# Order of the first loads in a two-layer attention and mixture-of-experts kernel

## Chip, core and metric

The kernel runs on one core of a Trainium2 chip. The metric is the device time of one execution in microseconds (us). The kernel before took 1843.43 us, the median of three runs (1840.93 to 1843.54).

## The reference, cut to what matters

Two layers run one after the other over 8 x 100 tokens of 512 features, all in float32. Each has cross attention to a context (722 rows for each of the 8 batches, 512 features) and a feed-forward part with 8 experts, of which every token takes 2. Only the first attention's beginning bears on the change:

```python
x = x + _L0_xattn_ref(_layernorm(x, axis=-1), ctx_1024, q_w, q_b, k_w, k_b, v_w, v_b, o_w, o_b)
# in _L0_xattn_ref(x, context, ...): 16 heads of 32
q = x @ q_w + q_b
k = context @ k_w + k_b
v = context @ v_w + v_b
att = einsum('bhtd,bhsd->bhts', q, k) / sqrt(32)
att = where(tril(ones((T, S))), att, -inf)      # causal: only the first 100 context rows count
y = einsum('bhts,bhsd->bhtd', softmax(att), v)
return y @ o_w + o_b
...
# then the experts of layer 0, attention of layer 1 (all 722 context rows), the experts of layer 1
```

Since a token sees at most the first 100 context rows in this first attention, the keys and values need only those rows.

## The kernel before, in words

The tokens lie in one tile `x`, in seven tiles of rows: the first holds 32, the other six 128 each. The context is handed over feature by feature, so that one piece of 128 features of the first 100 rows of all batches (`cT[:, dc]`, four pieces, 400 KB each) is 128 partitions with 8 runs of 100 numbers, 400 bytes each. The weights `k_w`, `q_w`, `v_w`, `o_w` are handed over so that each is one load of 128 partitions with 8 KB each (1 MB); they go through a ring of eight tiles (`Weights`, L43 to L63), whose loads all stand in SP's queue.

Instructions are issued by five engines, each in its own order; a planner (the tile framework's scheduler) lays out that order from the order of the program and the dependencies. A load is issued by the engine that the program names: SP and ACT have a hardware queue each, POOL (GpSimd) a software queue. In the order of the program:

- The tokens come first, in ACT's queue (L106 to L109): tile 0, tile 1, tiles 2 and 3, tiles 4 to 6.
- Constants follow: the identity, `eps`, `rank` and so on.
- In the first attention (from L515), the four pieces of `cT` go to SP, SP, POOL, POOL (L519, L520), then the four weights to SP (L522), then the small parameters through POOL (L523 to L529). Two of these are wide: `v_b` and `o_b`, spread over 128 partitions, 256 KB each (L524, helper L162).
- POOL then makes the mask and `nil`, a tile of zeros (L531 to L534). SP fills two tables in memory, `sent` and `answers`, with these zeros, 25 loads of 512 KB each (L535 to L543), with the loads of `Wm` and of the first context for later stages among them (L542, L544).
- TensorE begins with two parts of the key columns (`columns(0, 2)` and `columns(0, 3)`, L606 and L607; helper `columns_part`, L454): each sums four chunks `dc` of `cT` and `k_w`, and ScalarE evicts each with the bias `k_b` (L556).
- The seven token tiles are then normalised (L608 to L612): VectorE makes the moments (L133, L135), ScalarE the root (L153), VectorE the reciprocal, the shift and the scaled tile `xn` (L154, L156, L160), TensorE transposes it (L171), ScalarE copies it to `xT` (L173), and POOL adds `o_b` to `x` (L612).
- Two parts of the query columns follow (L613), and then the 32 units of the first attention (L627), with values, scores and softmax.

Of the kernel before, what the change touches and what calls it, by code (L numbers as in the profile page):

```python
# [8 lines left out]
F32 = mybir.dt.float32  # L9
# [4 lines left out]
P = 128  # L14
D = 512
# [4 lines left out]
NTILE = -(-NT // P)  # L20
# [19 lines left out]
SHORT = NT - NT // P * P  # L40
# [26 lines left out]
def two_layers(ctx: ExitStack, tc: tile.TileContext, a: dict, out: bass.AP):  # L67
    nc = tc.nc
    x_in = a["x"].rearrange("b t d -> (b t) d")
    y_out = out.rearrange("b t d -> (b t) d")  # L70
    rows = [SHORT] + [P] * (NTILE - 1)
    starts = [0] + list(range(SHORT, NT, P))
# [30 lines left out]

    x = const.tile([P, NTILE, D], F32, name="x")
    nc.vector.memset(x[:, 0, :], 0.0)
    nc.scalar.dma_start(out=x[:SHORT, 0, :], in_=x_in[:SHORT])  # L106
    for i0, i1 in ((1, 2), (2, 4), (4, NTILE)):
        of_tiles = x_in[starts[i0] : starts[i0] + (i1 - i0) * P]
        nc.scalar.dma_start(out=x[:, i0:i1, :], in_=of_tiles.rearrange("(i p) d -> p i d", p=P))  # L109

    ident = const.tile([P, P], F32, name="ident")
    make_identity(nc, ident)
# [12 lines left out]
    def param(name, shape, pool=const):  # L125
        t = pool.tile(shape, F32, name=f"p_{name}")
        nc.gpsimd.dma_start(out=t, in_=a[name])
        return t
# [9 lines left out]
    def factors(mv, tag, twice=False, by_power=False):  # L138


        r = small.tile([P, 1], F32, tag=f"r{tag}", name=f"r{tag}")
        if by_power:
            if twice:
                nc.gpsimd.tensor_scalar(r, mv[:, 1:], 1.0 + EPS, EPS * EPS, ALU.mult, ALU.add)
                nc.gpsimd.tensor_tensor(r, r, half, ALU.pow)
            else:
                nc.gpsimd.tensor_scalar(r, mv[:, 1:], EPS, None, ALU.add)
                nc.gpsimd.tensor_tensor(r, r, half, ALU.pow)
        else:
            if twice:  # L150
                nc.scalar.activation(r, mv[:, 1:], AF.Sqrt, bias=eps2, scale=1.0 + EPS)
            else:
                nc.scalar.activation(r, mv[:, 1:], AF.Sqrt, bias=eps)  # L153
            nc.vector.reciprocal(r, r)  # L154
        t = small.tile([P, 1], F32, tag=f"t{tag}", name=f"t{tag}")
        nc.vector.scalar_tensor_tensor(t, mv[:, :1], -1.0, r, ALU.mult, ALU.mult)  # L156
        return r, t
# [4 lines left out]
    def broadcast(name, shape, pool, tag):  # L162
        t = pool.tile(shape, F32, tag=tag, name=f"p_{name}")
        nc.gpsimd.dma_start(out=t, in_=a[name].partition_broadcast(P))
        return t
# [349 lines left out]
    with tc.tile_pool(name="a0", bufs=1) as ap, tc.tile_pool(name="a0w", bufs=3) as aw, tc.tile_pool(  # L515
        name="a0s", bufs=1, space=bass.MemoryType.PSUM
    ) as ps_s, tc.tile_pool(name="a0p", bufs=2, space=bass.MemoryType.PSUM) as ps:
        cT = ap.tile([P, DC, B, T], F32, tag="cT", name="cT")
        for dc, queue in enumerate((nc.sync, nc.sync, nc.gpsimd, nc.gpsimd)):  # L519
            queue.dma_start(out=cT[:, dc], in_=a["ctxT"][dc * P : (dc + 1) * P, :, :T])  # L520
        cTf = cT.rearrange("p c b t -> p c (b t)")
        w_k, w_q, w_v, w_o = (weights.get(k, 0) for k in range(4))  # L522
        q_b, k_b = param("q_b", [P, DC], ap), param("k_b", [P, DC], ap)  # L523
        v_b, o_b = broadcast("v_b", [P, D], ap, "v_b"), broadcast("o_b", [P, D], ap, "o_b")  # L524
        gamma0, beta0 = param("gamma", [P, DC]), param("beta", [P, DC])
        wg0, bg0 = param("Wg", [P, DC, NE]), param("bg", [1, NE])
        b1 = param("b1", [P, NE, F0 // P])
# [139 lines left out]
        for i in range(NTILE):  # L667
# [9 lines left out]
            r, t = factors(mv, "a")  # L677
# [35 lines left out]
    with f0, tc.tile_pool(name="f0w", bufs=2) as fw, tc.tile_pool(  # L713
        name="f0p", bufs=2, space=bass.MemoryType.PSUM
# [89 lines left out]
    with tc.tile_pool(name="a1", bufs=1) as ap, ExitStack() as later, tc.tile_pool(  # L804
        name="a1s", bufs=1, space=bass.MemoryType.PSUM
# [3 lines left out]
        w_q, w_k, w_v, w_m, w_o = (  # L809
            [weights.get(W_L1A + 2 * n + g, 0) for g in range(2)] for n in (0, 2, 3, 1, 4)  # L810
        )
# [158 lines left out]
        for i in range(NTILE):  # L970
            n = min(t0 + T for t0 in range(0, NT, T) if t0 + T >= starts[i] + rows[i]) // T * IC + 2
# [27 lines left out]
    with tc.tile_pool(name="f1", bufs=1) as fp, tc.tile_pool(name="f1w", bufs=2) as fw, tc.tile_pool(  # L999
        name="f1p", bufs=2, space=bass.MemoryType.PSUM  # L1000
# [150 lines left out]
```

## Time and profile before

| what | us |
|---|---|
| median of three runs | 1843.43 |
| the profiled execution's own time | 1848.14 |
| its span, from the first to the last instruction | 1846.2 |
| TensorE's matmuls busy (PE) | 1725.2, 93% of the span |
| VectorE (DVE), ScalarE (ACT), GpSimd (POOL) busy | 584.5, 458.1, 167.7 |
| last matmul of the first two key parts issued | 26.9 |
| first transposes of the tokens | 28.74 |

The profile is one execution taken by the hardware profiler; its times are from the start of the span. PE is TensorE's matmuls, PEld its loading of weights, SPq, ACTq and POOLq are the issuing of loads. A group such as `L459 PE MATMUL ps_col<-cT,w` names the line, engine, operation and tiles; each matmul of the program in float32 shows as two. The memory queues are named by number: q1 is SP's, q10 ACT's, q0 POOL's. In the share of 16 engines, 100% means that all sixteen memory engines of the core worked for the whole window.

### The profile page before, as it was taken

The numbers are of one execution on the slowest core, as the hardware profiler recorded it, in microseconds if no ns is written. First come the engines' busy times: TensorE is split into PE (matmuls) and PEld (weight loads), VectorE is DVE, ScalarE is ACT, GpSimd is POOL, SyncE is SP. The second block draws the span as 40 slices with busy tenths as digits, with TensorE's granted clock in tenths as the row PEclk, the third lists the DMA queues.
The fourth block names the chain that finished last, engine by engine and source line by source line (L and its number), as shares of the span: only waits on it lengthen the run. The fifth ranks groups of instructions, "written<-read, shape, count | busy, mean of one in ns | idle before, by whom it ended". The sixth has DMA issues, their size and how long they took to land.

```text
span 1846.2 us, 26502 instructions
## 1 busy us (share of the span) xinstructions
PE 1725.2 (93%) x10427; PEld 1306.3 (71%) x10427; DVE 584.5 (32%) x1489; ACT 458.1 (25%) x1370; POOL 167.7 (9%) x283
## 2 busy tenths in 40 slices
PE   4999899999999979999999999999999959999990
PEld 2455578999999845666666656666666649999990
DVE  3464520110111140355444414444444411111115
ACT  2365321111111131333333323323233310010110
POOL 4010210000000150000010000000000010030003
PEclk9999899999999989999999999999999979999995
DMA  9921284454555563032120110213010265465513
GB/s 368 413 76 58 81 336 168 168 191 173 201 199 223 186 212 135 25 98 65 33 71 5 7 33 7 38 16 49 5 6 4 28 227 196 163 222 200 197 59 116
DMA packets 74422, 233.32 MB, mean 126 GB/s; under 512 B 23178, under 2 KB 35582, under 8 KB 57894
## 3 DMA queue, kind: packets, MB, share of 16 engines
q1 hardware_dynamic: 52978, 183.42, 28.8%
q0 software_dynamic: 10128, 30.84, 5.2%
q10 hardware_dynamic: 11172, 17.17, 3.1%
q8 instruction: 86, 1.41, 0.3%
q14 instruction: 58, 0.48, 0.1%
HBM read 180.36 MB, written 51.04 MB: 125 GB/s over the span
## 4 chain that ended last, share of the span: by engine, by line
PE 62%; issue 15%; DMA 7%; POOL 1%; DVE 1%; ACT 1%; POOLq 0%; ACTq 0%; another core or an unknown queue 0%; SPq 0%; DVEq 0%
PE ps_m L470 14%; PE ps_h L734 10%; PE ps_y L399 9%; PE ps_sc L852 5%; PE ps_col L459 5%; PE ps_av L902 4%; PE ps_v L934 3%; PE ps_ptA L881 3%; DMA answers<-y 3%; PE ps_o L950 3%; PE ps_mv L482 2%; DMA firsts<-answers,where 1%; DMA back<-answers,where 1%; PE ps_tp L171 1%; ACT pr L858 1%
## 5 line engine op out<-in xcount | busy, mean ns | idle before, releaser
L470 PE MATMUL ps_m<-cb,w 128*128 128x361 f32 x896 | 297.5, 483 | 0.0
L399 PE MATMUL ps_y<-h,w 128*128 128x256 f32 (+7 forms) x1536 | 280.5, 344 | 0.0
L399 PEld LDWEIGHTS ps_y<-h,w 128*128 128x128 f32 x1536 | 268.6, 190 | 7.9
L470 PEld LDWEIGHTS ps_m<-cb,w 128*128 128x128 f32 x896 | 169.2, 194 | 102.5 <-issue 14.4
L734 PE MATMUL ps_h<-xgT,w 128*128 128x256 f32 (+7 forms) x1024 | 188.4, 345 | 0.0
L734 PEld LDWEIGHTS ps_h<-xgT,w 128*128 128x128 f32 x1024 | 179.9, 191 | 5.6 <-ACT h L738 0.2
L858 ACT ACTIVATE pr<-ps_sc,m 100x822 f32<-100x822 f32 x128 | 120.0, 943 | 187.8 <-DVE m L856 95.1
L856 DVE TENSOR_REDUCE m<-ps_sc 100x1 f32<-100x822 f32 x128 | 123.8, 1009 | 46.5 <-PE ps_sc L852 46.5
L474 ACT COPY mT<-ps_m 128x361 f32<-128x361 f32 x128 | 58.8, 462 | 311.1 <-PE ps_m L470 276.5
L882 DVE COPY prT<-ps_ptA 128x500 f32<-128x500 f32 x128 | 82.1, 678 | 168.4 <-PE ps_ptA L881 168.4
L738 ACT ACTIVATE h<-ps_h,s_b 128x256 f32<-128x256 f32 (+7 forms) x128 | 56.1, 439 | 303.5 <-PE ps_h L734 303.5
L459 PE MATMUL ps_col<-xT,w 128*128 128x400 f32 x320 | 113.2, 511 | 1.6 <-ACT xT L180 1.6
L1033 PE MATMUL ps_g<-xgT,w 128*128 128x256 f32 (+7 forms) x512 | 104.4, 347 | 0.0
L1033 PE MATMUL ps_u<-xgT,w 128*128 128x256 f32 (+7 forms) x512 | 102.8, 344 | 0.0
L459 PEld LDWEIGHTS ps_col<-xT,w 128*128 128x128 f32 x320 | 61.2, 195 | 46.9 <-issue 2.5
L1033 PEld LDWEIGHTS ps_g<-xgT,w 128*128 128x128 f32 x512 | 91.3, 192 | 3.0
L852 PE MATMUL ps_sc<-mT,qT 64*100 64x311 f32 (+1 forms) x512 | 93.1, 468 | 0.0
L1033 PEld LDWEIGHTS ps_u<-xgT,w 128*128 128x128 f32 x512 | 90.8, 190 | 2.7
L902 PEld LDWEIGHTS ps_av<-prT,mv 128*64 128x64 f32 (+1 forms) x1536 | 67.9, 137 | 27.1 <-issue 24.7
L1038 ACT ACTIVATE sg<-ps_g 128x256 f32<-128x256 f32 (+7 forms) x64 | 22.3, 349 | 238.8 <-PE ps_g L1033 238.8
L902 PE MATMUL ps_av<-prT,mv 128*64 128x100 f32 (+1 forms) x1536 | 80.6, 253 | 0.0
L881 PEld LDWEIGHTS ps_ptA<-ident,pr 100*128 100x128 f32 x640 | 65.2, 141 | 20.7 <-issue 10.5
(274 smaller groups left out, 1824.2 us busy)
## 6 DMA issues: line engine op xcount, KB each, us to landing
w<-in_W SPq DMA_DIRECT2D x64, 1024.0 KB
w<-in_w_gate SPq DMA_DIRECT2D x16, 1024.0 KB
w<-in_w_up SPq DMA_DIRECT2D x16, 1024.0 KB
w<-in_w_down SPq DMA_DIRECT2D x16, 1024.0 KB
sent<-nil SPq DMA_DIRECT2D x25, 512.0 KB
answers<-nil SPq DMA_DIRECT2D x25, 512.0 KB
cb<-in_ctxT ACTq DMA_DIRECT2D x16, 722.0 KB
mT<-kept_keys SPq DMA_DIRECT2D x13, 361.0 KB
```

The costliest lines, as they stand in the source:

```text
L399: nc.tensor.matmul(py[:, k, :n], ws[f // 4][:, f % 4, dc * P : (dc + 1) * P], h[:, f, :n], start=f == 0, stop=f == nf - 1,)
L459: nc.tensor.matmul(ps[:, :HALF], w[c // 4][:, dc, (c % 4) * P : (c % 4 + 1) * P], xT[:, dc, cols], start=dc == 0, stop=dc == DC - 1,)
L470: nc.tensor.matmul(pm[:, : S // 2], w_m[ic // 4][:, dc, (ic % 4) * P : (ic % 4 + 1) * P], cb[h][:, dc, : S // 2], start=dc == 0, stop=dc = ...
L474: nc.scalar.copy(mT[:, h * (S // 2) : (h + 1) * (S // 2)], pm[:, : S // 2])
L734: nc.tensor.matmul(ph[:, :n], w[:, dc, j * P : (j + 1) * P], xg[:, dc, :n], start=dc == 0, stop=dc == DC - 1,)
L852: nc.tensor.matmul(sc[:, bank, c0:c1], qT[r, ic, q0 : q0 + T], keys_, start=True, stop=True)
L856: nc.vector.tensor_reduce(m, sc[:, :, :NKH], AX.XY, ALU.max, negate=True)
L858: nc.scalar.activation(pr.rearrange("p (a n) -> p a n", a=2), sc[:, :, :NKH], AF.Exp, bias=m, accum_out=sums[:, j : j + 1],)
L881: nc.tensor.transpose(pt[:, c, :], pr[:, T + c * P : T + (c + 1) * P], ident[:T, :T])
L882: nc.vector.tensor_copy(prT[:, : NSC - 1, :], pt)
L902: nc.tensor.matmul(po[r, 0, :], vj, prT[j][:w, c, :], start=c == 0, stop=c == NSC)
L1033: nc.tensor.matmul(p_[:, :n], w_[:, dc, j * P : (j + 1) * P], xg[:, dc, :n], start=dc == 0, stop=dc == DC - 1,)
```

## The change

```diff
 x = const.tile([P, NTILE, D], F32, name="x")
 nc.vector.memset(x[:, 0, :], 0.0)
-nc.scalar.dma_start(out=x[:SHORT, 0, :], in_=x_in[:SHORT])
-for i0, i1 in ((1, 2), (2, 4), (4, NTILE)):
-    of_tiles = x_in[starts[i0] : starts[i0] + (i1 - i0) * P]
-    nc.scalar.dma_start(out=x[:, i0:i1, :], in_=of_tiles.rearrange("(i p) d -> p i d", p=P))
...
 cT = ap.tile([P, DC, B, T], F32, tag="cT", name="cT")
-for dc, queue in enumerate((nc.sync, nc.sync, nc.gpsimd, nc.gpsimd)):
+for dc, queue in enumerate((nc.sync, nc.scalar, nc.scalar, nc.scalar)):
     queue.dma_start(out=cT[:, dc], in_=a["ctxT"][dc * P : (dc + 1) * P, :, :T])
+nc.scalar.dma_start(out=x[:SHORT, 0, :], in_=x_in[:SHORT])
+for i0, i1 in ((1, 2), (2, 4), (4, NTILE)):
+    of_tiles = x_in[starts[i0] : starts[i0] + (i1 - i0) * P]
+    nc.scalar.dma_start(out=x[:, i0:i1, :], in_=of_tiles.rearrange("(i p) d -> p i d", p=P))
 cTf = cT.rearrange("p c b t -> p c (b t)")
 w_k, w_q, w_v, w_o = (weights.get(k, 0) for k in range(4))
 q_b, k_b = param("q_b", [P, DC], ap), param("k_b", [P, DC], ap)
-v_b, o_b = broadcast("v_b", [P, D], ap, "v_b"), broadcast("o_b", [P, D], ap, "o_b")
+v_b, o_b = (ap.tile([P, D], F32, tag=n, name=f"p_{n}") for n in ("v_b", "o_b"))
+for t, n in ((v_b, "v_b"), (o_b, "o_b")):
+    nc.gpsimd.tensor_copy(t[:1, :1], w_k[:1, 0, :1])
+    nc.gpsimd.dma_start(out=t, in_=a[n].partition_broadcast(P))
```

The first context piece stays in SP's queue, ahead of the weights; the other three go to ACT's queue, and the tokens behind them there. POOL's queue carries no context any more. The loads of `v_b` and `o_b` get a one-element copy from `k_w` ahead of them on POOL, which writes into the tile that the load fills: so each of the two loads waits until `k_w` has landed. What is computed stays the same.

The planner lays out the changed program with further differences: on ACT, the two evictions of the key columns stand ahead of all roots of the layer norm (before, five roots stood ahead of them), with one more table load between the evictions and the first root; on SP, the first piece of `Wm` stands behind the 25 fills of `sent` (before, ahead of them); the load of tokens 2 and 3 waits for `cT[:, 0]` and that of tokens 4 to 6 for `cT[:, 2]`, since they share semaphores with these.

## The prediction

> **What bounds the kernel now.** I read the page first, for the whole, and then only the first 46 us, since every edited line issues a first load. The row of slices, with the page's head:
>
> ```profile
> span 1846.2 us, 26502 instructions
> ...
> PE   4999899999999979999999999999999959999990
> ...
> PE 62%; issue 15%; DMA 7%; POOL 1%; DVE 1%; ACT 1%; POOLq 0%; ACTq 0%; another core or an unknown queue 0%; SPq 0%; DVEq 0%
> ```
>
> A slice is 46 us; in the first one TensorE is busy four tenths, and from then on nearly always. So the start is a stretch in which TensorE stands still, and from 36 us on (windows 36 to 46, 46 to 56 and 56 to 100 us show it 10.00, 9.94 and 43.93 us busy) it is the bound: a microsecond won or lost before 36.05 us is a microsecond of the end, unless a later wait eats it. The waits of the first 45 us, and then the order of time there:
>
> ```profile
> ACT ra L153 <- DVE mv_a L135: 20.3, 3, 10.5
> DVE st_a L133 <- DMA x<-in_x: 18.9, 3, 8.5
> PE ps_col L459 <- DMA w<-in_k_w: 18.8, 1, 18.8
> ```
>
> ```profile
> 3.28 1.28 ACT L153 ACT_TABLE_LOAD   x1 [3.28 <-DVE sel L235]
> ...
> 18.77 8.59 PE L459 MATMUL ps_col<-cT,w 128*128 128x400 f32 x16 [18.77 <-DMA w<-in_k_w]
> ...
> 25.81 0.69 DVE L133 BATCH_NORM_STATS2 st_a<-x 128x6 f32<-128x512 f32 x1 [7.71 <-DMA x<-in_x]
> ...
> 28.07 1.06 ACT L556 ACTIVATE kT<-ps_col,p_k_b 128x400 f32<-128x400 f32 x2
> ...
> 36.05 6.72 PE L459 MATMUL ps_col<-xT,w 128*128 128x400 f32 x16
> ```
>
> The columns are start, duration, engine, line, operation; in brackets the idle time and its end. The first view has total, times, longest: VectorE waits for tokens in three pieces, ScalarE for the moments that VectorE makes of them. TensorE waits 18.77 us for the keys' weights, makes the key columns until 27.36, then follows the layer norm of the seven token tiles (their last load landed at 25.8), and at 36.05 starts the query columns. **36.05 us is the number to move.** What shares the memory engines meanwhile:
>
> ```profile
> ## 3 DMA queue, kind: packets, MB, share of 16 engines
> q0 software_dynamic: 94, 0.34, 51.7%
> q10 hardware_dynamic: 102, 0.21, 32.9%
> q1 hardware_dynamic: 104, 0.10, 16.9%
> ```
>
> ```profile
> q1 hardware_dynamic: 201, 1.47, 90.9%
> ```
>
> ```profile
> q1 hardware_dynamic: 648, 0.25, 110.0%
> ```
>
> These are the queues between 7 and 9 us, SP's own queue (q1) between 20 and 24, and q1 between 4 and 5. In the first, three queues hold work, POOL's with records of some 4 KB, ACT's (q10) with 2 KB, SP's mostly with the 400-byte rows of cT, and each got the same number of records, about 100: **the turn goes by record, not by byte.** From the other two comes the price of a record on one of the 16 engines: 400 bytes 1.10 x 16 us / 648 = 27 ns; 8 KB 0.909 x 64 us / (1.47 MB / 8192) = 0.324 us.
>
> **The change, part by part.** A piece of cT is 128 x 8 rows of 400 bytes, so 64 records per engine; a weight matrix is 128 rows of 8 KB, so 8.
>
> *Context pieces.* Before, SP carried two and POOL two. Now SP carries cT0, then k_w, q_w, v_w, o_w; ACT carries cT1, cT2, cT3, then the tokens. In the changed program's order v_w waits for cT1's landing and o_w for k_w's, both early, so SP's queue does not run dry. Data start to flow at about 3 us (the rates by time show 46 GB/s up to 3 us, 280 after). cT0 and cT1 take turns: 128 x 27 ns = 3.5 us, to 6.5. Then k_w: 8 turns of 0.324 + 0.027 = 2.8 us, to 9.3, seen by TensorE at about 10. So far the plan holds, 8.7 us sooner than 18.77. But q_w, v_w and o_w follow with no wait, and for each of their 24 turns cT2 gets one 400-byte row. By the time SP's 32 big records are through, ACT's queue has moved 32 of its 128 rows. cT3 is in when everything ahead has gone: 256 x 27 ns = 6.9, 32 x 0.324 = 10.4, and v_b and o_b (0.52 MB, by the same price per byte) 1.3, in all 18.6; from 3 us that is 21.6, and with the way to the semaphore 22.5. cT2 comes 64 x 27 ns = 1.7 us earlier, at 20.8. Bounds: 12.5 us if nothing overtakes (3 + 6.9 + 8 x 0.324, all pieces and k_w alone), 25.8 if the slowest engine lags as it did for the last tokens.
>
> Here a rule is weighed. The Trainium skill (DMA: Bandwidth & Descriptors, Queues, rings and completion order) says an engine drains a whole packet, some 9 to 17 descriptors, from one row's ring before it turns to the next. With 13 rows for each 8 KB turn, cT2 and cT3 (128 rows) would need 10 turns, 10 x (0.324 + 13 x 0.027) = 6.8 us, and land at 13.3. POOL's 4 KB records in the trace look like such bundles; the hardware queues' 400-byte records do not, 104 against 102 and 94. I take the row.
>
> *Key columns.* They wait per piece: the first two of four chunks can run at 10 us, the third at 20.8, the fourth at 22.5. A chunk is two of the sixteen passes. Before, the first nine weight loads of the group stood 0.67 us apart and the rest about 0.33, after some 6 us of work; I take the same, counted from 20.8. From 22.5 ten passes are left: 6.4 slow ones to 26.8, 3.6 fast ones, 1.2 us, and 0.3 to drain: 28.3, against 27.36 before. **+0.9.**
>
> *ScalarE.* In the changed program's order both key evictions stand ahead of all seven square roots (L153); before, five roots came first, filling the wait. And there are now two table loads ahead of the roots where there was one, the second between the evictions and the first root. So: last eviction (0.58 plus a little) ends at 29.1, table 1.28, first root 0.3: 30.7. A load costs 1.28 by the row above; the skill (ScalarE: Activation LUTs, What ACT_TABLE_LOAD costs) adds a drain of 1.38, 2.66 in all. The load at 43.42 us started 0.02 us after the activation ahead of it ended, so no drain shows ahead of it; I take 1.28 and keep 1.4 for the range.
>
> *Layer norm.* Before, tiles 0 and 1 were normalised at 16.4 to 18.0 us under the wait for k_w, and tiles 2 to 6 took 25.81 to 35.03, 9.2 us, VectorE in order and some steps stretched to 1.2 to 1.5 us beside POOL's additions of o_b (L612, 1.27 each). Now all seven stand behind the roots: 9.2 + 1.6 = 10.8 us, to 41.5. The tokens are there: 50 records per engine of about 0.09 us behind cT3 end at 27 alone, and some 0.25 us a turn against the zero fills (their 4 KB records) gives 35, while the last three tiles are needed from about 34. Last transposes to query columns took 1.02 us (35.03 to 36.05): **42.5, +6.5 us.**
>
> *Wide biases behind k_w.* Two one-element copies on POOL wait for k_w at 10 us. Queued behind them: gamma, v_b, o_b, beta, Wg, bg, b1, ln_g, ln_b, w_router (0.54 us each), the mask, nil (0.97), the additions L612. SP's fills wait for nil (ready at 23.4 before; some 17 to 24 now), VectorE for v_b and mask at 46. Hidden; beyond 46 us each microsecond would count.
>
> *Wm.* Its first piece moves behind the 25 fills of sent on SP, 13 MB, some 31 us at 420 GB/s. It is first used at 137.5 us: hidden by 70 us.
>
> Nothing later is expected to eat the shift, since TensorE is dense to 200 us and the routing behind it is a serial chain. Sum: some +6.5, and +1 for what a lagging engine adds, **+7.5**. The profiled execution took 1848.1 (span 1846.2 and 1.9 around it), so 1855.6 there; the median of the runs shown is 4.7 lower, 1843.4, so 1851.
>
> **Rivals.** (1) *The pieces are not overtaken*, because rows go in bundles or are all in before q_w follows. Then everything is in at 12.5 to 13.3; key columns end at 21.1 to 21.9, the second table at 23.2 to 24, query columns 0.3 + 10.8 + 1.0 later: 35.3 to 36.1, **-0.8 to 0**. For it: the skill's rule, and k_w early; against: equal counts. Even here the gain is small, because the layer norm is no longer done under the wait. About 1843. (2) *Faster*: besides, the chain shrinks to VectorE's bare 8.9 us (7 x 0.86, three statistics, five aggregates), no addition colliding: 33.4 to 34.2, and the start at 10 that bytes alone would allow takes off 2 more: **-2 to -5**, 1840. (3) *Slower by more*: cT3 at 25.8 and the table at 2.66, query columns at 47, **+11**, 1854.5; it decides once cT3 lands after 24.
>
> **How the numbers follow.** Within 0.2% means 3.7 us, about what a measurement of this kernel can tell from no change. Main case with (3): 0.74, of which nearly all is beyond 3.7 us; (1) 0.20; (2) 0.06. So slower 0.73, same 0.21, faster 0.06. The likeliest alone ranges from 1847 to 1856; to reach 8 in 10, rival (1) has to be taken in part: 1842 to 1857.
>
> **What would show it.** In the changed profile: the first chunks of the key columns at about 10 us, then a TensorE gap to about 21 ended by cT; equal record counts of q1 and q10 between 8 and 20 us; a table load between the key evictions and the first root, at about 29; the query columns at 42 to 45. If the key columns run without a gap from 13 us, the starvation is wrong and so is the sign. If the query columns start late and the span does not grow, some later wait ate it.

## The result, and the profile after

| | us | against the kernel before on the same chip |
|---|---|---|
| kernel before, 5 runs | 1843.43 (1839.93 to 1848.24) | |
| changed kernel, 5 runs | 1850.03 (1848.37 to 1853.84) | 1.0029, 95% interval 1.0016 to 1.0043 |
| changed kernel once more, on another chip, 6 runs | 1851.82 (1850.03 to 1852.49) | 1.0045 (1.0032 to 1.0057) |

The change makes the kernel slower, by 5 to 8 us; 1851 was forecast. The profiled execution took 1853.84 us, its span 1851.9.

The page of the changed kernel, its head, the slices of TensorE, its granted clock and the chain:

```profile
span 1851.9 us, 26504 instructions
...
PE   4999989999999979999999999999999959999990
...
PEclk7999989999999979999999999999999979999995
...
PE 42%; issue 30%; DMA 10%; POOL 2%; DVE 1%; ACT 1%; POOLq 0%; ACTq 0%; DVEq 0%
```

The row of slices keeps its 4 at the start: a slice is 46 us, too coarse for a loss of some 7, and since every edited line issues a first load, the loss is looked for in the first 46 us. The chain says less: its share of "issue" doubled (15% before) and that of TensorE fell from 62% to 42%, while TensorE was busy 93% of the span in both; over the whole span the chain can run through other steps of a dense program, and the loss is not read from it. The granted clock of the first slice reads 7 where it read 9; more of that in the last section.

The waits of the first 46 us (total, times, longest), and the order of time there:

```profile
PE ps_col L455 <- DMA w<-in_k_w: 9.9, 1, 9.9
...
PE ps_col L455 <- DMA cT<-in_ctxT: 7.9, 1, 7.9
```

```profile
9.87 3.00 PE L455 MATMUL ps_col<-cT,w 128*128 128x400 f32 x4 [9.87 <-DMA w<-in_k_w]
20.80 7.13 PE L455 MATMUL ps_col<-cT,w 128*128 128x400 f32 x12 [7.92 <-DMA cT<-in_ctxT]
...
27.96 0.59 ACT L560 ACTIVATE kT<-ps_col,p_k_b 128x400 f32<-128x400 f32 x1 [3.50 <-PE ps_col L455]
28.57 1.28 ACT L149 ACT_TABLE_LOAD   x1
29.87 0.48 ACT L149 ACTIVATE ra<-mv_a,eps 128x1 f32<-128x1 f32 x2
...
43.56 7.26 PE L455 MATMUL ps_col<-xT,w 128*128 128x400 f32 x16
```

The wait for the keys' weights is halved, 18.77 to 9.87, and a new one stands in its place: after four passes TensorE stands still for 7.92 us, for a context piece. Then come the last eviction, the second table load, the first roots, and 13.7 us after the first root the query columns, at 43.56 instead of 36.05. The queues between 8 and 12 us (records, MB, share of 16 engines):

```profile
q1 hardware_dynamic: 226, 1.59, 94.9%
q10 hardware_dynamic: 224, 0.09, 8.4%
```

The same number of records, and 18 times the bytes: SP's weights in 8 KB records, ACT's context in 400-byte rows. Nothing behind it eats the shift: the first matmul of the values is 8.0 us later than before, that of `Wm` (137.5 us before) 8.1, the first of the experts (251.7) 7.9, the last of the program 6.6.

### The profile page after: what moved, and what is told of

It is laid out like the page before. It is cut to its first block, busy times and chain, and to the rows that moved or that the text cites. A ratio compares the mean times of both kernels' runs of the same rounds, so it can differ in the third digit from the quotient of the medians.

```text
span 1851.9 us, 26504 instructions
## 1 busy us (share of the span) xinstructions
PE 1728.8 (93%) x10427; PEld 1307.6 (71%) x10427; DVE 587.3 (32%) x1489; ACT 459.3 (25%) x1371; POOL 166.2 (9%) x283
## 3 DMA queue, kind: packets, MB, share of 16 engines
q8 instruction: 86, 1.41, 0.3%
## 4 chain that ended last, share of the span: by engine, by line
PE 42%; issue 30%; DMA 10%; POOL 2%; DVE 1%; ACT 1%; POOLq 0%; ACTq 0%; DVEq 0%
PE ps_m L466 14%; DMA answers<-y 7%; PE ps_sc L856 5%; PE ps_col L455 5%; PE ps_av L906 4%; PE ps_v L938 3%; PE ps_ptA L885 3%; PE ps_o L954 3%; PE ps_mv L478 2%; DMA back<-answers,where 1%; DMA xg<-sent 1%; ACT pr L862 1%; PE ps_ptB L889 1%; PE ps_ptB L888 1%; PE ps_tp L167 1%
## 5 line engine op out<-in xcount | busy, mean ns | idle before, releaser
L466 PEld LDWEIGHTS ps_m<-cb,w 128*128 128x128 f32 x896 | 168.2, 193 | 101.3 <-issue 12.3
L906 PEld LDWEIGHTS ps_av<-prT,mv 128*64 128x64 f32 (+1 forms) x1536 | 68.4, 137 | 27.9 <-issue 25.4
```

Of the source, the lines that this page charges most:

```text
L466: nc.tensor.matmul(pm[:, : S // 2], w_m[ic // 4][:, dc, (ic % 4) * P : (ic % 4 + 1) * P], cb[h][:, dc, : S // 2], start=dc == 0, stop=dc = ...
L906: nc.tensor.matmul(po[r, 0, :], vj, prT[j][:w, c, :], start=c == 0, stop=c == NSC)
```

## The experiments

Each ratio is to the kernel before on the same chip; the runs were made on several chips. "Values" is the shift of the first matmul of the values (42.6 us before), behind both query parts; the last column is (ratio - 1) x 1844 us.

| run | query columns, us | values | ratio (95%) | us |
|---|---|---|---|---|
| changed kernel | 43.56 | +8.0 | 1.0029 (1.0016 to 1.0043) | +5.3 |
| e5: changed kernel again | 42.66 | +6.8 | 1.0045 (1.0032 to 1.0057) | +8.3 |
| e1: weights wait for context | 33.26 | -1.6 | 0.9992 (0.9986 to 0.9999) | -1.5 |
| e2: roots on POOL | 41.57 | +6.0 | 1.0045 (1.0031 to 1.0058) | +8.3 |
| e3: one table load | 41.46 | +6.4 | 1.0050 (1.0037 to 1.0064) | +9.2 |
| e4: context in long rows | 39.99 | +4.4 | 1.0023 (1.0012 to 1.0033) | +4.2 |
| e6: wide biases free | 43.26 | +7.6 | 1.0033 (1.0020 to 1.0046) | +6.1 |
| e7: stream divided | 28.22 | -7.3 | 0.9967 (0.9959 to 0.9976) | -6.1 |
| e8: e7, late additions | 27.31 | -9.8 | 0.9954 (0.9941 to 0.9967) | -8.5 |
| e9: before, late additions | 31.19 | -5.9 | 0.9978 (0.9970 to 0.9986) | -4.1 |
| e10: e1, late additions | 28.63 | -7.5 | 0.9962 (0.9948 to 0.9976) | -7.0 |
| e11: e10, VectorE evicts | 27.74 | -8.6 | 0.9940 (0.9923 to 0.9957) | -11.1 |
| e12: e10, long rows | 24.48 | -12.3 | 0.9921 (0.9908 to 0.9935) | -14.6 |

Over all thirteen the time follows the start within 3 us, where the intervals reach 1.2 to 3.1 us to either side: what the first 46 us win or lose is, as far as these times can tell, what the kernel wins or loses. A start is read from one execution: the two profiles of the changed kernel differ by 0.9 us at the query columns and by 1.2 at the values, so a start is uncertain by about 1 us.

### e1: is it the overtaking? The other weights wait for the last context piece

```diff
-        w_k, w_q, w_v, w_o = (weights.get(k, 0) for k in range(4))
+        w_k = weights.get(0, 0)
+        weights.load(4, cT[:1, 3, 0, :1])
+        w_q, w_v, w_o = weights.tiles[1:4]
...
-        weights.load(W_LATE)
+        weights.load(W_LATE, cT[:1, 3, 0, :1])
```

> The changed kernel, but the loads of q_w, v_w, o_w and Wm wait until the last context piece has landed; the late roots and the second table load stay. Overtaking by record (my theory): cT2 and cT3 have only k_w's 8 big records beside them, so the last piece lands at 13 to 14 us (20.8 and later in the changed kernel), the key columns run from 10 us with hardly a gap and end at about 20, the first root is at about 22.5, and the query columns start 13.7 us later (as in the changed kernel, 29.87 to 43.56), at about 36: total 7 us below the changed kernel, level with the one before. Rival (it is the bytes ahead, or the slow 400-byte rows themselves, not the turns): the gap to about 20 us stays, and the total stays within 2 us of the changed kernel. Rival (only the late roots cost): the key columns end early, but the query columns stay after 41.

In its timeline the gap is gone, and its queues between 8 and 12 us show why:

```profile
9.87 7.76 PE L455 MATMUL ps_col<-cT,w 128*128 128x400 f32 x16 [9.87 <-DMA w<-in_k_w]
...
19.57 0.48 ACT L149 ACTIVATE ra<-mv_a,eps 128x1 f32<-128x1 f32 x2
...
33.26 7.94 PE L455 MATMUL ps_col<-xT,w 128*128 128x400 f32 x16
```

```profile
q10 hardware_dynamic: 1895, 0.94, 99.8%
q1 hardware_dynamic: 48, 0.26, 15.8%
```

ACT's queue moves 1895 records where it moved 224; the key columns end at 17.6 instead of 27.9, and the query columns start 10.3 us sooner than in the changed kernel's first profile, 9.4 sooner than in e5's. That is 2.7 us earlier than forecast, because the key columns end at 17.6 and not at 20. So the overtaking costs some 10 us at the start and more than all of the loss. Without it the new order is worth only 1.5 us (interval 0.2 to 2.6): the roots still stand behind both evictions, and from the first root (19.57) to the query columns it is 13.7 us again.

### e2 and e3: do the late roots and the second table load cost?

```diff
-            scaled(xn, x[:, i, :], *factors(moments(x[:, i, :], "a0"), "a"))
+            scaled(xn, x[:, i, :], *factors(moments(x[:, i, :], "a0"), "a", by_power=True))
```

> The changed kernel, but the seven roots of the first layer norm are taken on POOL (two small operations a tile) and no longer on ScalarE, so they don't stand behind the key evictions and the second table load goes; the loads stay as in the changed kernel. If the late roots carry their part of the cost: the key columns still end at about 28, tiles 0 to 2 are scaled by then (tokens land at 22 to 26), and the query columns start at 36 to 38 and not at 43.6, total 5 to 7 us below the changed kernel. If the overtaken context pieces carry it all: the first transposes still wait for the evictions at 28.6 and the tiles go through one at 1.6 us after another, query columns at 40 to 43, total 0 to 3 us below.

```diff
+        first = ap.tile([P, 1], F32, name="first_root")
+        nc.scalar.activation(first, eps, AF.Sqrt)
```

> The changed kernel with one square root of a constant ahead of the key evictions, so that ScalarE loads the table with the root first and needs no second load between the evictions and the roots. By the row (1.28 us): the first root 1.3 us earlier, the query columns at about 42.3, total 1.3 us lower, which the times can hardly show. By load and drain (2.66): the query columns at about 40.9. If the load is hidden: no shift of the query columns.

In e2 POOL takes the roots, and the first transposes follow the key columns at once, at 26.68, 3.7 us sooner than in e5. But POOL's power (0.57 us each) stands in line with its additions (1.27 to 1.36 each), a pair of tiles takes 4.9 us, and the query columns start at 41.57, only 1.1 us sooner than in e5, in the range that was forecast for no part of the late roots: but the chain changed its pace-maker, so e2 leaves open what late roots cost by themselves. e3 is cleaner. An early root loads the table before it is needed, and ScalarE's timeline has no load behind the second eviction:

```profile
27.29 0.59 ACT L562 ACTIVATE kT<-ps_col,p_k_b 128x400 f32<-128x400 f32 x1 [3.02 <-PE ps_col L455]
27.79 0.47 ACT L149 ACTIVATE ra<-mv_a,eps 128x1 f32<-128x1 f32 x2
```

From the start of the eviction to that of the root it is 0.50 us; in the changed kernel 29.87 - 27.96 = 1.91. The load was worth 1.41 us, close to its row of 1.28 and far from the 2.66 of the Trainium skill (ScalarE: Activation LUTs, What ACT_TABLE_LOAD costs). In the total neither run shows: 1.0045 and 1.0050 beside e5's 1.0045, with starts only 1.1 to 1.2 us sooner than e5's, less than the intervals resolve.

### e4: the same bytes in rows of 3,200 bytes

```diff
-            queue.dma_start(out=cT[:, dc], in_=a["ctxT"][dc * P : (dc + 1) * P, :, :T])
+            queue.dma_start(out=cT[:, dc].rearrange("p b t -> p (b t)"), in_=a["ctx0"][dc * P : (dc + 1) * P])
...
+        "ctx0": i["ctx_1024"][:, :T].transpose(2, 0, 1).reshape(D, NT),
```

> The changed kernel with the context's first 100 rows handed over as an input of their own, so that a piece of cT is 128 partitions with one run of 3200 bytes: the same bytes in the same queues, an eighth of the records (8 per engine and piece). Turns by record: cT2 needs only 8 turns beside k_w and cT3 8 beside q_w, so they land at about 9.5 and 13 us and the key columns run from 10 to 20; the planner then also puts roots ahead of the second eviction and has one table load; the tokens, still behind SP's big records, land until about 24.7, and the query columns start at about 35: total 7 to 9 us below the changed kernel. Turns by bytes or the order of the queue as such: cT2 at 20.8 as before and the total unchanged.

A piece is now 8 records per engine instead of 64, on the same queues in the same order, with the same weights beside it. Its timeline, the key columns and the statistics of token tiles 2 and 3, and of 4:

```profile
9.59 7.41 PE L455 MATMUL ps_col<-cT,w 128*128 128x400 f32 x16 [9.59 <-DMA w<-in_k_w]
...
22.44 1.29 DVE L129 BATCH_NORM_STATS2 st_a<-x 128x6 f32<-128x512 f32 x2 [6.82 <-DMA x<-in_x]
29.42 0.69 DVE L129 BATCH_NORM_STATS2 st_a<-x 128x6 f32<-128x512 f32 x1 [3.01 <-DMA x<-in_x]
```

The row length alone takes the gap away: the turn goes by record. But the last tokens, 2 KB records behind the context in the same queue, are in at 29.4 and not at 24.7, and the query columns start at 39.99, where 35 was forecast; the total gained 1 to 4 us instead of 7 to 9. From 20 to 24 us, while the tokens are waited for, the queues show the same turn again:

```profile
q1 hardware_dynamic: 160, 1.18, 74.9%
q10 hardware_dynamic: 161, 0.32, 21.2%
q0 software_dynamic: 160, 0.09, 7.4%
```

The starvation moved down the queue, and +7.5 became +3.9.

### e5 and e6: the wide biases' wait

```diff
-        for t, n in ((v_b, "v_b"), (o_b, "o_b")):
-            nc.gpsimd.tensor_copy(t[:1, :1], w_k[:1, 0, :1])
-            nc.gpsimd.dma_start(out=t, in_=a[n].partition_broadcast(P))
+        v_b, o_b = broadcast("v_b", [P, D], ap, "v_b"), broadcast("o_b", [P, D], ap, "o_b")
```

> The changed kernel once more, unchanged, so that the other variants of it have it on their own chip. Both theories: 1.002 to 1.005 of the kernel before. If it lies at 1.004 to 1.005, the variants whose query columns start 2 us earlier gained nothing that the total shows; if it lies at 1.002 to 1.003, they lost 2 to 4 us somewhere behind the start.

> The changed kernel with the wide biases' loads free to go at once, as in the kernel before. Theory (a turn goes by record): the biases' 4 KB records join the turn early, 8 per engine at about 0.16 us each, so that the keys' weights are complete about 1.3 us later (TensorE starts near 11.2 instead of 9.9), the third and fourth context pieces land within 1 us of 20.8, query columns at 43 to 44.5, total within 1 us of the changed kernel: the biases' wait is not where the time went. Rival (the wait is what costs, through the layer norms' additions on POOL): query columns 2 us or more earlier and the total 2 us or more lower.

The key columns of e6, and then of e5:

```profile
10.69 3.00 PE L455 MATMUL ps_col<-cT,w 128*128 128x400 f32 x4 [10.69 <-DMA w<-in_k_w]
20.37 7.25 PE L455 MATMUL ps_col<-cT,w 128*128 128x400 f32 x12 [6.68 <-DMA cT<-in_ctxT]
```

```profile
9.82 3.01 PE L455 MATMUL ps_col<-cT,w 128*128 128x400 f32 x4 [9.82 <-DMA w<-in_k_w]
20.60 6.43 PE L455 MATMUL ps_col<-cT,w 128*128 128x400 f32 x12 [7.77 <-DMA cT<-in_ctxT]
```

On the same chip, TensorE got the keys' weights at 10.69 us without the wait and at 9.82 with it, so the wait does bring them 0.9 us sooner (1.3 was forecast). It buys nothing that shows: the next context piece comes at 20.37 against 20.60, and 1.0033 and 1.0045 lie in each other's intervals.

### e7 and e8: the stream divided over both queues, and the additions late

```diff
-        for dc, queue in enumerate((nc.sync, nc.scalar, nc.scalar, nc.scalar)):
+        for dc, queue in enumerate((nc.sync, nc.sync, nc.scalar, nc.scalar)):
...
-        for i0, i1 in ((1, 2), (2, 4), (4, NTILE)):
+        w_k = weights.get(0, 0)
+        for (i0, i1), queue in (((1, 2), nc.scalar), ((2, 4), nc.scalar), ((4, NTILE), nc.sync)):
...
-            nc.scalar.dma_start(out=x[:, i0:i1, :], in_=of_tiles.rearrange("(i p) d -> p i d", p=P))
+            queue.dma_start(out=x[:, i0:i1, :], in_=of_tiles.rearrange("(i p) d -> p i d", p=P))
```

> The changed kernel with the stream divided over both queues: two context pieces, the keys' weights and the last three token tiles on SP's queue, the other two context pieces and the first four token tiles on ScalarE's. Theory (the short rows starve because all of them stand behind one queue's 8 KB records): context in by about 14, keys and tokens by about 17.6, key columns without a long gap, five roots in front of the key evictions, query columns at about 30.5 (-5.5 against the kernel before), total about 5 us below the kernel before, ratio 0.997. Rival (what comes early at the head is given back behind it): query columns near 30 but a total within 2 us of the kernel before. Rival (turns do not go by record): landings as late as in the changed kernel, query columns above 40.

For e8 besides: the load of `o_b` waits for the query columns, and its seven additions to `x` stand behind them.

```diff
-            nc.gpsimd.tensor_tensor(x[:, i, :], x[:, i, :], o_b, ALU.add)
         for part in range(2):
             columns(0, part)
+        nc.gpsimd.tensor_copy(o_b[:1, :1], qT[:1, 0, :1])
+        nc.gpsimd.dma_start(out=o_b, in_=a["o_b"].partition_broadcast(P))
+        for i in range(NTILE):
+            nc.gpsimd.tensor_tensor(x[:, i, :], x[:, i, :], o_b, ALU.add)
```

> As the divided stream, and the output bias's load and its seven additions to the token tiles moved behind the query columns, so that POOL does not work beside VectorE in the layer norms. Theory (the 13.7 us from the first root to the query columns are VectorE's operations drawn out beside POOL's additions): the chain shrinks to about 10 to 11 us, query columns at about 28, total about 8 us below the kernel before, ratio 0.9955. Rival (the chain is paced by VectorE's own work or by the hand-over to TensorE): query columns within 1 us of the divided stream's.

e7's queues between 8 and 12 us, and its two groups of columns:

```profile
q10 hardware_dynamic: 486, 0.66, 57.4%
q1 hardware_dynamic: 502, 0.69, 52.9%
```

```profile
14.79 7.38 PE L455 MATMUL ps_col<-cT,w 128*128 128x400 f32 x16 [14.79 <-DMA w<-in_k_w]
...
28.22 7.23 PE L455 MATMUL ps_col<-xT,w 128*128 128x400 f32 x16
```

Nearly equal records again, and now nearly equal bytes, since each queue carries two context pieces first and long rows behind them. The keys' weights come 4.9 us later than in the changed kernel, the query columns 15.3 us sooner and 2.3 sooner than forecast: the tokens are in before the key columns end, and the planner has five roots ahead of the evictions. The last-named rival, landings as late as in the changed kernel, is gone; so is the one that something later takes it back. e8 adds 2.4 us in the total, a little more than the 0.9 at the start of the query columns, because these then run in 5.64 instead of 7.23 us. The 0.9 lies within the 1 us that the forecast had named as the sign of its rival, so e8's start doesn't settle what the additions cost; in e7 they had drawn out only two of VectorE's steps (to 1.08 and 1.38 us). The next runs settle it.

### e9, e10, e11: the layer norm's chain

e9 is the kernel before with e8's late additions alone, e10 is e1 with them. In e11 VectorE evicts the first two key parts:

```diff
+                (lambda o, i: nc.vector.tensor_scalar(o, i, bias[:, c : c + 1], None, ALU.add))
+                if c == 0 and part > 1 else
```

> The kernel before, with none of the change, and only the output bias's load and its seven additions moved behind the query columns. Theory (POOL's additions draw VectorE's normalizations out from 0.55 to 1.46 us, whatever the order of the first loads): four drawn-out operations of the tail lose some 0.6 to 1.1 us each, query columns at about 33 instead of 36.05, total 2 to 4 us below the kernel before, ratio about 0.998. Rival (the gain of the late additions in the divided stream came only from its own order of instructions): query columns within 1 us of 36, ratio 1.000.

> As the variant whose other weights wait for the third context piece's neighbour at the end of the context (key columns end at 17.6, first root at 19.6), with the additions moved behind the query columns. Theory: the 13.7 us from the first root to the query columns shrink as VectorE is no longer drawn out, to about 8 us (seven tiles at about 1.1 us), query columns at about 27.5, total 7 to 9 us below the kernel before, ratio 0.996. Rival (the chain is paced by the root's round over ScalarE and VectorE, not by the drawn-out operations): 11 us or more, query columns at 31 or later.

> As the run before it, and the first two key evictions made by VectorE instead of ScalarE, which leaves the roots free of them and saves one table load. Theory: tokens are in by 14.4, five of seven roots taken before the key columns end, so that behind their end at 17.6 only transposes and copies are left (about 4.5 us, as in the divided stream with late additions): query columns at 22 to 23, total 12 to 15 us below the kernel before, ratio about 0.993. Rival (the query weights, held back until 12.4, land only then): TensorE waits for them, query columns at 24 to 27. Rival (what starts earlier meets the later weights' loads further on): query columns as forecast, the total no lower than the late variant of the divided stream.

From the first root to the query columns e1 took 33.26 - 19.57 = 13.7 us, e10 28.63 - 19.28 = 9.35. The order of ScalarE and VectorE is nearly the same; what is gone is POOL's addition beside VectorE, with the load of `o_b`. The changed kernel's timeline, POOL and VectorE, over the middle and the end of the chain:

```profile
36.94 0.66 DVE L129 BATCH_NORM_STATS2 st_a<-x 128x6 f32<-128x512 f32 x1
36.95 1.27 POOL L616 TENSOR_TENSOR x<-x,p_o_b 128x512 f32<-128x512 f32 x1 [0.36 <-DVE ra L150]
...
38.97 1.27 POOL L616 TENSOR_TENSOR x<-x,p_o_b 128x512 f32<-128x512 f32 x1 [0.75 <-DVE ta L152]
39.06 1.45 DVE L156 TENSOR_SCALAR xn<-x,ra,ta 128x512 f32<-128x512 f32 x1
...
40.60 1.26 POOL L616 TENSOR_TENSOR x<-x,p_o_b 128x512 f32<-128x512 f32 x1 [0.36 <-DVE ra L150]
40.62 1.25 DVE L152 SCALAR_TENSOR_TENSOR ta<-mv_a,ra 128x1 f32<-128x1 f32 x1
```

Beside an addition of 1.27 us the scaled tile takes 1.45 instead of 0.55, and the shift `ta`, one number per partition, 1.25 instead of 0.15: the shift ends with the addition (41.87 and 41.86), the scaled tile 0.27 us behind it. The statistics are not touched (0.66). The Trainium skill states such a rule (SBUF — State Buffer, Who interferes with whom): a VectorE instruction with two inputs from that memory contends with one of GpSimd that reads it, one with a single input does not (outside modes that use both ports). The rows agree with it in kind: `ta` reads two tiles, the statistics one. The scaled tile reads one tile and two numbers per partition; which of these collides, no run here tells. In e10's timeline the same steps are short:

```profile
19.28 0.48 ACT L149 ACTIVATE ra<-mv_a,eps 128x1 f32<-128x1 f32 x2
...
25.26 0.55 DVE L156 TENSOR_SCALAR xn<-x,ra,ta 128x512 f32<-128x512 f32 x1
...
26.90 0.55 DVE L156 TENSOR_SCALAR xn<-x,ra,ta 128x512 f32<-128x512 f32 x1
...
28.63 6.63 PE L455 MATMUL ps_col<-xT,w 128*128 128x400 f32 x16
```

e10's total lies 7.0 us below the kernel before, at the low end of the forecast, but the chain is 9.35 us and not 8; the root's round over two engines is a part of it (VectorE stands 0.58 us for a root at 25.18). e9 gained more at the start than forecast (31.19 against 33). One microsecond of it is the keys' weights, at 17.77 instead of 18.77, since `o_b`'s load no longer stands ahead of them; this was not in the forecast. e11's place was missed: 27.74 instead of 22 to 23, though its total, -11.1 us, is only a little short of the 12 to 15 forecast. The planner put two roots, not five, ahead of the key columns' end, and VectorE's second eviction (18.55) ahead of the first scaled tile (19.10); behind it the next three tiles came 1.33 us apart, the last three 0.9 to 1.25. The query weights were not what was waited for: the columns start at once behind the last transposes (26.86).

### e12: three measures together

> Three measures together: the other weights wait for the context, the context's pieces lie in rows of 3,200 B as an input of their own, and the additions of the output bias stand behind the query columns. ScalarE's order has four roots in front of the second key eviction and one table load. Theory: key columns from 9.8 to about 17.3, three normalized tiles ready by then, behind them seven transposes and copies with the last tiles' normalization: query columns at 22 to 24, total 12 to 14 us below the kernel before, ratio 0.993. Rival (the last three tiles' statistics and roots come only behind the evictions, as in the run where VectorE evicts the keys): query columns at 26 to 28, total as in that run, 10 to 11 us below, ratio 0.994.

The edits of e1, e4 and e8's additions together. Its timeline:

```profile
8.59 7.06 PE L455 MATMUL ps_col<-cT,w 128*128 128x400 f32 x16 [8.59 <-DMA w<-in_k_w]
...
24.48 5.95 PE L455 MATMUL ps_col<-xT,w 128*128 128x400 f32 x16
```

Half a microsecond later than forecast, and the total is 14.6 us below the kernel before (interval 12.0 to 17.0): faster than the kernel before and the changed one. It hands the first 100 context rows over a second time, in another layout; where that is not wanted, e8 (-8.5 us) and e11 (-11.1) beat both kernels without it.

## Why the prediction was right

- **The turn goes by record: right.** 226 and 224 records in 8 to 12 us; e4's edit changed nothing but the row length and the gap went, e1's nothing but what overtakes. The skill's rule that was weighed (DMA: Bandwidth & Descriptors, Queues, rings and completion order) would have had the context in at 13.3; on these two queues the measurement decides against it. The sign named, equal counts from 8 to 20 us, held to 16 (180 and 184 from 12 to 16); from 16 to 20 ACT moved 951 records against SP's 80, since SP's weights were nearly through.
- **Keys' weights at 10, third piece at 20.8, fourth at 22.5: right.** 9.87, 20.80, and the fourth released its weight load at 21.82, before TensorE's passes came to it. The key columns ended at 27.93, forecast 28.3.
- **Evictions, table, first root: right, 0.5 early.** Eviction at 28.55 (29.1), first root done at 30.16 (30.7). The load alone is 1.41 us by e3.
- **The layer norm's chain: mis-sized.** Forecast 10.8 us from the first root to the last scaled tile, measured 30.16 to 42.53, 12.4. The forecast took over the five tiles of before with their drawn-out steps (9.2 us) and gave the other two 1.6 us at bare length; but with all seven in one line three scaled tiles (1.52, 1.45, 1.45) and three shifts (0.71, 0.71, 1.25) are drawn out, 5.0 us in all over their bare lengths of 0.55 and 0.15; before, two of each (1.19, 1.46; 0.37, 1.25), 2.9 us. e1 against e10 measures the collision at 4.3 us.
- **+1 for a lagging engine: not seen.** It stood in the sum for the wrong thing: 42.5 + 1 and 43.56 agree because the chain was 1.6 longer and the first root 0.5 earlier than worked out. That they agree so closely is luck: e5, the same kernel, starts the query columns at 42.66.
- **Wide biases and `Wm` hidden: right.** e6, and a shift of 8.0 at the values and 8.1 at `Wm`'s first use.
- **Nothing later eats it: right to 1.4 us** (6.6 of 8.0 left at the last matmul; in e5 5.0 of 6.8, while e5's total is 8.3 longer).
- **Rival (1)**, no overtaking, had 1843 and no gain; e1 made it real: -1.5 us. Its total held on two errors that cancel in part: key columns end at 17.6, not 21.1 to 21.9, since they need not wait for the last piece before they start, and the chain of 12.1 us is 13.7.
- **Rival (2)** had named what was left in the change: a chain with no addition colliding. With the overtaking gone too it is worth more than its 2 to 5 us: 7.0 in e10.

What stays open: what late roots cost by themselves (e2 exchanged one pace-maker for another), and why e11 and e12 gained 2 to 3 us more in the total than at the values, which their intervals (3.1 and 2.5 us to either side) hardly tell from nothing.

## What to carry to other kernels

Before a load is put into a queue with short rows, count records, not bytes: beside a queue of 8 KB records a queue of 400-byte rows moves one row a turn, so either nothing long may stand beside it (a wait), or both queues carry short rows first and long ones behind them, or the rows are made longer. A first operand that comes sooner is worth only what the last operand of the same stage allows; ask which wait ends last after the change. Work that nobody needs yet (here POOL's additions) can sit on the path by drawing out another engine's short steps, and moving it behind the stage, with the load that it needs, paid 4 us in the unchanged kernel (e9).

## What the runs showed of the hardware

**TensorE's first passes behind a standstill are slow.** The weight loads of consecutive passes stand 0.67 us apart at first and 0.33 later. In the kernel before they stand 0.67 apart from 18.74 to 24.84 in the key columns; in the changed kernel again behind the gap, to 26.30, and once more at the head of the query columns, to 46.90. e5 has the same two stretches, to 24.76 and 45.33. Where the transposes follow each other closely, in e8 and e9, the sixteen passes of the query columns have no slow stretch and take 5.64 us; in the kernel before they took 6.72, in the changed one 7.26 and 6.91 (e5), and in e1, which has no gap in its key columns, 7.94. So the layer norm's scattered transposes are enough. In the changed kernel this makes 0.5 us of difference to before, the step from +7.5 at the query columns to +8.0 at the values; in e5 0.2.

**The granted clock in the profile shows only a part of this.** Windows of the changed kernel: window, length, busy us of PE, PEld, DVE, ACT and POOL, then the granted clock, the memory engines' share and GB/s:

```profile
9.80:13.00 3.20, 3.00 (x4) 1.17 (x4) 0.00 (x0) 0.00 (x0) 3.20 (x8) 1.00 1.02 416
13.00:20.80 7.80, 0.00 (x1) 0.00 (x1) 0.00 (x0) 0.00 (x0) 3.67 (x8) 0.71 1.08 346
20.80:24.00 3.20, 3.20 (x5) 1.80 (x6) 1.64 (x4) 1.41 (x2) 0.00 (x0) 0.50 1.06 356
...
28.00:43.50 15.50, 6.85 (x28) 4.92 (x29) 12.09 (x29) 6.94 (x15) 8.48 (x7) 0.56 1.03 419
43.50:52.00 8.50, 8.50 (x22) 4.44 (x21) 0.00 (x0) 2.31 (x4) 0.91 (x2) 0.79 1.03 420
```

The four passes ahead of the gap took 3.00 us at a recorded 1.00, the first four behind it 3.04 at 0.50. And the fall inside the gap is not what the gap does each time: in e5, the same kernel with the same gap, and in e2, e3 and e6 with gaps of 6.7 to 7.7 us, the record reads 1.00 through the gap and through the key columns behind it, and 0.50 only from 31 to 33 us on, in the layer norm. What sets the moment is not shown, and a single profile's clock is no measure of what a gap costs.

**A queue that is overtaken also holds the engine that fills it.** ScalarE's loads of the tokens in the changed kernel:

```profile
3.60 13.05 ACTq L518 DMA_DIRECT2D x<-in_x  x1
...
16.70 4.45 ACTq L521 DMA_DIRECT2D x<-in_x  x3
```

Issuing these four took ScalarE until 21.15 us; in the kernel before its four token loads were issued by 3.24, in e4, with the long rows, by 6.38, and in e1, without the overtaking, by 9.81. Here it cost nothing, since ScalarE's first eviction waited for TensorE until 23.87; but no root could have been taken before then.

Not every drawn-out step lies beside an addition: in e8 two scaled tiles took 2.52 us from 17.12, where the same pair took 1.00 in e2, while POOL issued loads and filled tiles. They lay under the key columns and cost nothing; the cause is open.
